# Selective-scan layer of a four-layer image network: softplus operations of POOL moved behind the products of their unit, three buffers for h and two for its product with C

## The chip, the cores and the metric

The kernel runs on one core of a Trainium2 chip, in one launch. The metric is the device time of that launch in microseconds, as the median of several runs. The engines are called as the profile calls them: PE (TensorE), DVE (VectorE), ACT (ScalarE), POOL (GpSimd) and SP (SyncE, which here only issues DMAs).

## What is computed

The network has four layers, each of the form `x = x + layer(group_norm(x))`, on `x` of shape 2 x 192 x 96 x 96 in float32: a deformable convolution, a Laplacian with a 1x1 convolution, a bidirectional RWKV recurrence, and a selective scan. Only the last one is touched. Cut to what matters, it is this, with L = 9216 places in a row per image, 384 inner channels and 16 states per channel:

```python
xz = x_flat @ W_in.T                       # 192 -> 768
x_in, z_gate = split(xz, 2)
x_conv = silu(causal_conv4(x_in) + conv_b) # 4 taps per channel
dt, B_ssm, C_ssm = split(W_x @ x_conv, [12, 28])
delta = softplus(W_dt @ dt + 2 * b_dt)
A = -exp(A_log)
# for every place t, channel d, state n:
h = exp(delta * A) * h + (delta * x_conv) * B_ssm
y = sum_n(h * C_ssm) + D * x_conv
out = W_out @ (y * silu(z_gate))
```

## The kernel before

The place axis is cut into 38 steps (19 per image: 17 of 511 places and two of 264 or 265). The work of a step on the recurrence is cut into 12 **units**, numbered q = 0 to 11: three blocks of 128 channels (index i), each in four parts (index v). A unit holds 32 channels x 16 states, as 128 partitions (16 states by 8 channels) with 4 rows in the free dimension (index r). So a loop over k = 0 to 455 runs over all units, with step s = k // 12 and q = k % 12.

Work on a unit, with the lines of the kernel:

- `load` (L2336, SP): a 1022 KB DMA brings `delta * x_conv` from the DRAM tensor `ud`, repeated over the states, into `bu` (pool `sc`, four buffers). ACT copies the state that the step before left into its first column (L2340).
- `times_b` (L2346, POOL): `bu` times the row of B, in place.
- `steps_of` (L2356, PE): four small matmuls spread delta over the states into PSUM banks `da`. There are five such banks for four rows, so those of unit q+1 need banks that the scan of unit q frees.
- `decay` (L2370, ACT): `da = exp(A * delta)`, in place in PSUM, four operations.
- `scan` (L2379, DVE): four `tensor_tensor_scan` operations write `h` (pool `sb`, two buffers) from `da` in PSUM and `bu`.
- `times_c` (L2403, DVE): rows 0 to 2 of `h` times the row of C in PSUM, into `hc` (pool `s3`, three buffers).
- `times_c_aside` (L2414, POOL): row 3 of `h` times the same row in SBUF, into `hp` (pool `s3`).
- `sum_of` (L2427, PE): sums `hc` and `hp` over the states into the PSUM bank `acc`; at v = 0 it begins with the term of D (L2421).
- `gate` (L2440, DVE), after each fourth unit: `acc` times the gate.
- `keep` (L2386, ACT): the last column of `h` becomes the state.

Beside the units, three generators make the rest, one piece at each call of `go`. `early(s + 2)` makes normalization, input projections (L2242), convolution (L2262) and SiLU for two steps ahead. `late(s + 1)` makes the small projections, softplus and `ud` for the next step. `output(s - 1)` makes the output projection (L2452) and adds the residual (`xr`, L2460). Their matmuls share one PSUM bank, `pe`, so that each waits for the copy of the one before.

The softplus part of `late` is `relu(a) + log(1 + exp(-|a|))` with a correction for rounding. After ACT's Exp (L2310) and the addition of one (L2311), the pieces are: one of DVE (L2313) with ACT's Ln behind it (L2314), and then three of POOL, each on 128 x 1533 elements:

```python
nc.vector.scalar_tensor_tensor(du, ln, -1.0, du, ALU.add, ALU.subtract)   # L2313
nc.scalar.activation(ln, ln, AF.Ln)                                       # L2314
yield
nc.gpsimd.tensor_tensor(ln, ln, du, ALU.subtract)                         # L2316
yield
nc.gpsimd.tensor_tensor(dl, dl, ln, ALU.add)                              # L2318
yield
nc.gpsimd.tensor_tensor(du, dl, us, ALU.mult)                             # L2320
```

L2320 is followed by four DMAs from SP that write `ud` (L2322), which the loads of the next step read.

The order on PE, ACT, DVE and POOL is the order in which the program is written (`manual_schedule`); SP's order is the framework's. In iteration k the loop writes: `sum_of(k - 2)`, `scan(k)`, `steps_of(k + 1)`, `decay(k + 1)`, `times_c(k)`, `gate` if due, at q = 4 to 7 a piece of `late`, then `times_c_aside(k - 1)`, `times_b(k + 2)`, `load(k + 3)` and `keep(k)`, with pieces of the generators between by tables (`AHEAD`, `BEHIND`). Counting the calls, the piece with L2313 and Ln falls on q = 4, and those with L2316, L2318 and L2320 on q = 5, 6 and 7. On POOL the order of units 5 to 7 is therefore: the softplus operation, `hp` of unit q - 1, `times_b` of unit q + 2.

Of the kernel before, what the change touches and what calls it, by code (L numbers as in the profile page):

```python
# [6 lines left out]
F32 = mybir.dt.float32  # L7
# [11 lines left out]
P = 128  # L19
# [44 lines left out]
class Net:  # L64
# [2021 lines left out]
    def layer3(self, x, out, stats):  # L2086
# [4 lines left out]
        TM = 511  # L2091
# [8 lines left out]
        with ExitStack() as ctx:  # L2100
            wp = ctx.enter_context(tc.tile_pool(name="w3", bufs=1))
            s1 = ctx.enter_context(tc.tile_pool(name="l3s", bufs=1))
            sb = ctx.enter_context(tc.tile_pool(name="l3", bufs=2))
            s3 = ctx.enter_context(tc.tile_pool(name="l3h", bufs=3))
# [102 lines left out]
            steps = []  # L2207
# [120 lines left out]
            def where(k):  # L2328
                return k // NQ, k % NQ, k % NQ // NV, k % NV
# [13 lines left out]
            def times_b(k):  # L2343
                s, q, _, _ = where(k)
                bu = got[s]["bu", q][:, :, 1:]
                nc.gpsimd.tensor_tensor(  # L2346
                    bu, bu, got[s]["bs"].unsqueeze(1).to_broadcast([P, 4, steps[s][2]]), ALU.mult
                )

            def steps_of(k):  # L2350
                s, q, i, v = where(k)
                T = steps[s][2]
                das = [decays[(4 * k + r) % 5][:, : T + 1] for r in range(4)]
                for r in range(4):
                    at = slice(32 * r, 32 * r + 32)
                    nc.tensor.matmul(  # L2356
                        das[r][:, 1:],
                        spread[at, v].rearrange("p n e -> p (n e)"),
                        got[s]["dl"][at, i],
                        start=True,  # L2360
                        stop=True,
                        tile_position=(32 * r, 0),
                    )
                got[s]["da", q] = das

            def decay(k):
                s, q, _, _ = where(k)
                for r in range(4):
                    da = got[s]["da", q][r][:, 1:]
                    nc.scalar.activation(  # L2370
                        da, da, AF.Exp, scale=nA[:, 4 * q + r : 4 * q + r + 1]
                    )

            def scan(k):
                s, q, _, _ = where(k)
                h = sb.tile([P, 4, TM + 1], F32, name="h")[:, :, : steps[s][2] + 1]
                bu = got[s]["bu", q]
                for r in range(4):
                    nc.vector.tensor_tensor_scan(  # L2379
                        h[:, r], got[s]["da", q][r], bu[:, r], 0.0, ALU.mult, ALU.add  # L2380
                    )
                got[s]["h", q] = h

            def keep(k):
                s, q, _, _ = where(k)
                nc.scalar.copy(state[:, q], got[s]["h", q][:, :, steps[s][2]])  # L2386

            def rows_c(s):
                cc = ps.tile([P, TM], F32, name="cc")[:, : steps[s][2]]
                nc.tensor.matmul(  # L2390
                    cc,
                    pick.rearrange("p n e -> p (n e)"),
                    got[s]["xd"][:NST],
                    start=True,
                    stop=True,
                )
                got[s]["cc"] = cc

            def times_c(k):
                s, q, _, _ = where(k)  # L2400
                T = steps[s][2]
                hc = s3.tile([P, 3, TM], F32, name="hc")[:, :, :T]
                nc.vector.tensor_tensor(  # L2403
                    hc,
                    got[s]["h", q][:, :3, 1:],
                    got[s]["cc"].unsqueeze(1).to_broadcast([P, 3, T]),
                    ALU.mult,
                )
                got[s]["hc", q] = hc

            def times_c_aside(k):
                s, q, _, _ = where(k)
                hp = s3.tile([P, TM], F32, name="hp")[:, : steps[s][2]]
                nc.gpsimd.tensor_tensor(hp, got[s]["h", q][:, 3, 1:], got[s]["cs"], ALU.mult)  # L2414
                got[s]["hp", q] = hp

            def sum_of(k):
                s, q, i, v = where(k)
                if v == 0:
                    acc = ps.tile([P, TM], F32, name="acc")[:, : steps[s][2]]  # L2420
                    nc.tensor.matmul(  # L2421
                        acc, skip[:, i], got[s]["us"][:, i], start=True, stop=False
                    )
                    got[s]["acc"] = acc
                acc = got[s]["acc"]
                for r in range(4):
                    nc.tensor.matmul(  # L2427
                        acc[32 * r : 32 * r + 32],
                        gather[:, v],
                        got[s]["hc", q][:, r] if r < 3 else got[s]["hp", q],  # L2430
                        start=False,
                        stop=v == NV - 1,
                        tile_position=(0, 32 * r),
                    )

            def gate(k):
                s, q, i, v = where(k)
                if i == 0:
                    got[s]["y"] = s1.tile([P, ND, TM], F32, name="y")[:, :, : steps[s][2]]
                nc.vector.tensor_tensor(  # L2440
                    got[s]["y"][:, i], got[s]["acc"], got[s]["zs"][:, i], ALU.mult
                )

            def output(s):
                b, t0, T = steps[s]
                y = got[s]["y"]
                xr = s1.tile([CH, 2, TM], F32, name="xr")[:, :, :T]
                nc.sync.dma_start(out=xr, in_=halves(x[b])[:, :, t0 : t0 + T])
                for m in range(2):
                    pe = bank(T)  # L2450
                    for d in range(ND):
                        nc.tensor.matmul(  # L2452
                            pe[:CH],
                            w_out[:, d, m * CH : (m + 1) * CH],
                            y[:, d],
                            start=d == 0,
                            stop=d == ND - 1,
                        )
                    yield
                    nc.vector.tensor_tensor(xr[:, m], pe[:CH], xr[:, m], ALU.add)  # L2460
                    if m == 1:
                        nc.sync.dma_start(out=halves(out[b])[:, :, t0 : t0 + T], in_=xr)
                    yield
# [29 lines left out]
            def go(name):  # L2493
                next(running[name], None)

            for k in range(nk):
                s, q, _, _ = where(k)
                if q == 0 and s + 1 < ns:
                    running["late"] = late(s + 1)
                if q == 2 and s:  # L2500
                    running["out"] = output(s - 1)
                if q == 3 and s + 2 < ns:
                    running["early"] = early(s + 2)
                if q in AHEAD:
                    go(AHEAD[q])
                    go(AHEAD[q])
                if k >= 2:
                    sum_of(k - 2)
                if q == 0 and s:
                    rows_c(s)  # L2510
                scan(k)
                if q in (4, 5):
                    go("out")
                if k + 1 < nk:
                    steps_of(k + 1)
                if q in BEHIND:
                    go(BEHIND[q])
                if k + 1 < nk:
                    decay(k + 1)
                if q in BEHIND and BEHIND[q] != "out":  # L2520
                    go(BEHIND[q])
                if q == 3:
                    go("late")
                    go("early")
                times_c(k)
                if k >= 2 and (k - 2) % NV == NV - 1:
                    gate(k - 2)
                if q in (4, 5, 6, 7):
                    go("late")
                if q == 11:  # L2530
                    go("early")
                if k:
                    times_c_aside(k - 1)
                if k + 2 < nk:
                    times_b(k + 2)
                if k + 3 < nk:
                    load(k + 3)
                keep(k)
# [99 lines left out]
```

## Time and profile before

| | |
|---|---|
| median of 3 runs | 10368.99 us (10358.51 to 10370.72) |
| the profiled execution, its own time | 10352.81 us |
| span of its instructions | 10351.0 us, mean granted clock 0.915 |
| busy share PE, DVE, ACT, POOL | 88%, 79%, 59%, 67% |
| first and last scan (L2379) start | 7137.2 and 10341.5 us |
| in the stretch 7137 to 10343: PE, DVE, POOL, ACT busy | 3013, 2848, 2835, 1993 of 3206 us |
| in the same stretch: granted clock, DMA share | 0.89, 0.77 |

All times of rows are microseconds from the start of the span, unless marked ns. A row of the page's list of groups gives line, engine, operation, `out<-in`, shapes and count; then the busy time and the mean in ns of one; then the idle time of the engine just before these instructions and what ended most of it. A row of a timeline gives start, duration, engine, line, operation, names, shapes and count of neighbours merged; in brackets stand the engine's idle time before it and what ended that. A row of windows gives the stretch, its length, busy time and count of PE, its weight loads, DVE, ACT and POOL, and then the granted TensorE clock, the DMA share and GB/s.

### The profile page before, as it was taken

What the parts mean: (1) busy time and instruction counts of PE and PEld (TensorE: products, weight loads), DVE (VectorE), ACT (ScalarE), POOL (GpSimd) and SP (SyncE); (2) the same over time, 40 slices, a digit from 0 to 9 for tenths busy, and PEclk for the clock granted to TensorE, in tenths of its full rate; (3) what the DMA queues carried; (4) which work ended last, traced back from release to release, by engine and by line L of the source; (5) the groups of instructions that cost most, each with busy time, mean ns of one, the idle gap of its engine ahead of it and who ended that gap; (6) DMA issues with size and microseconds to landing.
All of it is one profiled execution on the core that took longest, in us unless ns stands there. A gap on an engine that the chain in (4) does not pass through costs nothing. (4 is left out here: it accounts for less than half of the span.)

```text
span 10351.0 us, 222379 instructions
## 1 busy us (share of the span) xinstructions
PE 9158.5 (88%) x87686; PEld 5342.5 (52%) x87686; DVE 8210.6 (79%) x8842; ACT 6081.6 (59%) x11850; POOL 6980.6 (67%) x5645
## 2 busy tenths in 40 slices
PE   4799999999979999999866777887999999999998
PEld 3587788787768888888722222223222222222223
DVE  5688878788677777777655789984889888888888
ACT  0366666666667677777500168664666666666665
POOL 1466666766666666666511268773888889988898
PEclk8899999999989999999978788887999999988898
DMA  8455555555434555555444344433787777878776
GB/s 148 91 139 135 136 136 139 137 136 134 119 90 128 136 136 138 139 137 138 109 131 129 117 149 159 130 118 83 172 176 172 172 174 173 173 173 172 174 170 149
DMA packets 877164, 1465.17 MB, mean 142 GB/s; under 512 B 251616, under 2 KB 682276, under 8 KB 875012
## 3 DMA queue, kind: packets, MB, share of 16 engines
q1 hardware_dynamic: 663276, 1264.09, 48.9%
q0 software_dynamic: 104000, 133.19, 5.8%
q10 hardware_dynamic: 108840, 53.57, 2.1%
q8 instruction: 701, 11.49, 0.5%
q14 instruction: 347, 2.84, 0.1%
HBM read 871.06 MB, written 381.46 MB: 121 GB/s over the span
## 5 line engine op out<-in xcount | busy, mean ns | idle before, releaser
L2379 DVE TENSOR_TENSOR_SCAN h<-da,bu 128x512 f32<-128x512 f32 (+2 forms) x1824 | 1981.6, 1148 | 374.0 <-POOL hp L2414 200.1
L581 DVE TENSOR_TENSOR sp<-h 128x2304 f32<-128x2304 f32 x790 | 2165.0, 2773 | 41.6 <-ACT h L560 41.6
L2346 POOL TENSOR_TENSOR bu<-bu,bs 128x2044 f32<-128x2044 f32 (+2 forms) x456 | 1958.3, 4295 | 66.0 <-DMA bu<-ud 53.0
L605 ACT COPY st<-pt 128x512 f32<-128x512 f32 (+1 forms) x2370 | 1213.6, 515 | 1100.8 <-PE pt L597 1029.4
L597 PE MATMUL pt<-ident,sp 128*128 128x128 f32 x14220 | 1674.8, 276 | 87.4 <-DVE sp L581 41.0
L603 DVE COPY st<-pt 128x512 f32<-128x512 f32 x1580 | 1063.7, 687 | 829.9 <-PE pt L597 810.7
L597 PEld LDWEIGHTS pt<-ident,sp 128*128 128x128 f32 x14220 | 1565.3, 142 | 169.9 <-issue 97.2
L551 POOL TENSOR_TENSOR h<-u,step 128x1152 f32<-128x1152 f32 (+1 forms) x474 | 1096.0, 2330 | 679.8 <-DVE u L524 480.8
L569 POOL DMA_DIRECT2D xw<-xp_d x2500 | 1389.9, 619 | 194.7 <-PE pt L648 82.5
L2370 ACT ACTIVATE da<-da,nA 128x511 f32<-128x511 f32 (+2 forms) x1824 | 1063.4, 638 | 595.0 <-PE da L2356 586.9
L648 PE MATMUL pt<-st,xw 64*32 64x288 f32 (+1 forms) x30000 | 1098.0, 371 | 141.8 <-DVE st L603 62.7
L674 ACT COPY val<-pt 128x288 f32<-128x288 f32 (+1 forms) x3000 | 958.0, 404 | 285.2 <-PE pt L648 259.9
L776 PE MATMUL pf<-main,wd 126*64 126x128 f32 (+1 forms) x17064 | 986.2, 274 | 9.7 <-DMA far_m<-val 9.4
L776 PEld LDWEIGHTS pf<-main,wd 126*64 126x64 f32 x17064 | 913.7, 140 | 155.9 <-issue 146.9
L2356 PE MATMUL da<-dl,spread 32*128 32x511 f32 (+2 forms) x3648 | 984.0, 643 | 6.7 <-DVE h L2379 6.7
L648 PEld LDWEIGHTS pt<-st,xw 64*32 64x32 f32 x30000 | 548.0, 107 | 556.6 <-ACT val L674 171.7
L2403 DVE TENSOR_TENSOR hc<-h,cc 128x1533 f32<-128x1533 f32 (+2 forms) x456 | 751.2, 1647 | 0.0
L797 PE MATMUL pf<-more,wl 118*64 118x144 f32 (+5 forms) x11592 | 737.9, 278 | 3.0 <-DMA more<-far_l 2.2
L797 PEld LDWEIGHTS pf<-more,wl 118*64 118x64 f32 (+1 forms) x11592 | 670.2, 137 | 71.1 <-issue 63.4
L2356 PEld LDWEIGHTS da<-dl,spread 32*128 32x128 f32 x3648 | 311.6, 192 | 674.7 <-DVE h L2379 396.1
L2414 POOL TENSOR_TENSOR hp<-h,cs 128x511 f32<-128x511 f32 (+2 forms) x456 | 553.4, 1214 | 99.6 <-DVE h L2379 48.1
L2242 PE MATMUL pe<-xn,sb_w_in 96*128 96x511 f32 (+2 forms) x912 | 527.1, 709 | 94.6 <-ACT xi L2250 37.1
(344 smaller groups left out, 13016.1 us busy)
## 6 DMA issues: line engine op xcount, KB each, us to landing
bu<-ud SPq DMA_DIRECT2D x408, 1022.0 KB
main<-val SPq DMA_DIRECT2D x2016, 91.1 KB
far_l<-val SPq DMA_DIRECT2D x288, 324.0 KB
xw<-xp_d POOLq DMA_DIRECT2D x2500, 26.0 KB
far_m<-val SPq DMA_DIRECT2D x288, 162.0 KB
half_d<-hv SPq DMA_DIRECT2D x54, 768.0 KB
hv<-half_d SPq DMA_DIRECT2D x54, 768.0 KB
more<-far_l SPq DMA_DIRECT2D x576, 60.8 KB
```

What stands on the lines that cost most here:

```text
L551: nc.gpsimd.tensor_tensor(hs, u[:, :, 8 * KK * l : 8 * KK * l + n].unsqueeze(3).to_broadcast([P, 2, n, WS]), con["step"].unsqueeze(1).unsq ...
L569: nc.gpsimd.dma_start(out=xw[e * WN : (e + 1) * WN, i], in_=xp_d[y : y + WS, x : x + WS, e * CM // 2 : e * CM // 2 + XW],)
L581: nc.vector.tensor_tensor(sp.rearrange("p s (y x) -> p s y x", x=WS), hy.unsqueeze(3).to_broadcast([P, n, WS, WS]), hx.unsqueeze(2).to_bro ...
L597: nc.tensor.transpose(pt[:, q], sp[:, 2 * (q0 + q) : 2 * (q0 + q) + 2].rearrange("p e w -> p (e w)"), self.ident,)
L603: nc.vector.tensor_copy(st[:, q0 : q0 + m], pt[:, :m])
L605: nc.scalar.copy(st[:, q0 : q0 + m], pt[:, :m])
L648: nc.tensor.matmul(to, xw[e * WN : (e + 1) * WN, win, g * CG : g * CG + 32], sts[pair][e * WN : (e + 1) * WN].rearrange("p s (r c) -> p s ...
L776: nc.tensor.matmul(place(cv, m, 2 - t // 3, 2 - t % 3, None, 0), con["wd"][:, cv, t, m * CO : (m + 1) * CO], blocks(took, 1, rows), start= ...
L797: nc.tensor.matmul(place(cv, m, 2 * cv if alone else 1 - cv, 2 - t, h, 1 - alone,), con["wl"][lanes, slot, t, m * CO : (m + 1) * CO], bloc ...
L2346: nc.gpsimd.tensor_tensor(bu, bu, got[s]["bs"].unsqueeze(1).to_broadcast([P, 4, steps[s][2]]), ALU.mult)
L2356: nc.tensor.matmul(das[r][:, 1:], spread[at, v].rearrange("p n e -> p (n e)"), got[s]["dl"][at, i], start=True, stop=True, tile_position=( ...
L2379: nc.vector.tensor_tensor_scan(h[:, r], got[s]["da", q][r], bu[:, r], 0.0, ALU.mult, ALU.add)
```

## The change

The tile `h` comes from the pool with three buffers and `hc` from the one with two. At q = 4 nothing moves; at q = 5, 6 and 7 the piece of `late` is written behind `times_c_aside(k - 1)` and `times_b(k + 2)` and ahead of `load(k + 3)`. No instruction is added or removed.

```diff
             def scan(k):
                 s, q, _, _ = where(k)
-                h = sb.tile([P, 4, TM + 1], F32, name="h")[:, :, : steps[s][2] + 1]
+                h = s3.tile([P, 4, TM + 1], F32, name="h")[:, :, : steps[s][2] + 1]
...
             def times_c(k):
                 s, q, _, _ = where(k)
                 T = steps[s][2]
-                hc = s3.tile([P, 3, TM], F32, name="hc")[:, :, :T]
+                hc = sb.tile([P, 3, TM], F32, name="hc")[:, :, :T]
...
                 times_c(k)
                 if k >= 2 and (k - 2) % NV == NV - 1:
                     gate(k - 2)
-                if q in (4, 5, 6, 7):
+                if q == 4:
                     go("late")
                 if q == 11:
                     go("early")
                 if k:
                     times_c_aside(k - 1)
                 if k + 2 < nk:
                     times_b(k + 2)
+                if q in (5, 6, 7):
+                    go("late")
                 if k + 3 < nk:
                     load(k + 3)
                 keep(k)
```

## The prediction

> **What bounds the kernel now.** I read the page first, then the timelines of single engines through one step of the last layer, then two stretches with the granted clock. The page:
>
> ```profile
> span 10351.0 us, 222379 instructions
> ...
> DVE  5688878788677777777655789984889888888888
> ...
> L2379 DVE TENSOR_TENSOR_SCAN h<-da,bu 128x512 f32<-128x512 f32 (+2 forms) x1824 | 1981.6, 1148 | 374.0 <-POOL hp L2414 200.1
> ```
>
> The last layer is the last 12 slices, and DVE is the busiest there beside PE. Its scan idled 374.0 us, 200.1 of them because POOL had not finished hp of two units earlier: with two buffers, scan of unit q may not overwrite h before hp of unit q-2 has read it. I write S5 for the scan of unit 5 of a step, and likewise hp4, times_b7, hc4. Now DVE in one step of twelve units (S0 at 8322.94, next S0 at 8412.59), and POOL beside it:
>
> ```profile
> 8350.57 4.56 DVE L2379 TENSOR_TENSOR_SCAN h<-da,bu 128x512 f32<-128x512 f32 x4
> 8355.17 0.69 DVE L2460 TENSOR_TENSOR xr<-pe,xr 96x511 f32<-96x511 f32 x1
> 8355.78 1.74 DVE L2403 TENSOR_TENSOR hc<-h,cc 128x1533 f32<-128x1533 f32 x1
> 8357.44 1.75 DVE L2313 SCALAR_TENSOR_TENSOR du<-ln,du 128x1533 f32<-128x1533 f32 x1
> 8359.10 4.56 DVE L2379 TENSOR_TENSOR_SCAN h<-da,bu 128x512 f32<-128x512 f32 x4
> 8363.58 0.66 DVE L2460 TENSOR_TENSOR xr<-pe,xr 96x511 f32<-96x511 f32 x1
> ...
> 8376.23 4.57 DVE L2379 TENSOR_TENSOR_SCAN h<-da,bu 128x512 f32<-128x512 f32 x4 [2.87 <-POOL hp L2414]
> ...
> 8385.30 4.57 DVE L2379 TENSOR_TENSOR_SCAN h<-da,bu 128x512 f32<-128x512 f32 x4 [2.86 <-POOL hp L2414]
> ```
> ```profile
> 8350.89 4.52 POOL L2346 TENSOR_TENSOR bu<-bu,bs 128x2044 f32<-128x2044 f32 x1 [0.47 <-DMA bu<-ud]
> 8362.48 3.43 POOL L2316 TENSOR_TENSOR ln<-ln,du 128x1533 f32<-128x1533 f32 x1 [7.07 <-ACT bu L2340]
> 8365.87 1.25 POOL L2414 TENSOR_TENSOR hp<-h,cs 128x511 f32<-128x511 f32 x1
> 8367.09 4.50 POOL L2346 TENSOR_TENSOR bu<-bu,bs 128x2044 f32<-128x2044 f32 x1
> ```
>
> S4, S5, S7 and S8 are shown. In unit 5 POOL stands 7.07 us: the softplus subtraction L2316 is ahead of hp4 and times_b7 and needs ACT's Ln (8360.92 to 8362.40), which needs DVE's L2313. Then each of units 5 to 7 has a 3.4 us softplus operation ahead of its hp, and S6, S7, S8 wait 0.66, 2.87 and 2.86. In 34 steps that is 200 us.
>
> What ends last after xr of unit 5 (done at 8364.24) is another thing: a PE and ACT sequence through one PSUM bank, project, copy, project, copy, taps, with the decays between, up to S1 of the next step (8420.21). PE waits for DVE only where it needs a bank of da that a scan frees:
>
> ```profile
> 8364.29 3.11 PE L2242 MATMUL pe<-xn,sb_w_in 96*128 96x511 f32 x4 [0.58 <-DVE xr L2460]
> ...
> 8377.28 3.58 PE L2356 MATMUL da<-dl,spread 32*128 32x511 f32 x8
> ...
> 8384.01 3.77 PE L2242 MATMUL pe<-xn,sb_w_in 96*128 96x511 f32 x4 [0.67 <-ACT zs L2257]
> ```
>
> So a step is two pieces in series: DVE without a gap from S2 to xr of unit 5, then PE and ACT from xr to the next S1. Steps come in three kinds in turn, 86.3, 86.9 and 89.7 us (mean 87.6), with tails from xr of 53.7, 53.4 and 56.0 us.
>
> **Part 1: h with three buffers, hp ahead of softplus.** S7 then waits for hp4, done at about 8356.7. All 200 us of waits for hp go, but in the tail only what PE waits for counts. In the step from 8236.63 this is one place, L2356 for unit 9 at 8297.73: 3.41 us where a free one takes 1.14. That is 2.27, of which 0.44 is lost again because the next copy then waits for ACT's decays: 1.83. In the step from 8149.78 the same place took 2.80: 1.66 less 0.49, 1.17. In the step shown it is the 3.58 above: 2.44. There the granted clock was half from 8382.1 to 8388.9, after that wait, and cost more: the L2242 before and at 8384.01 took 2.54 and 3.77 against 1.98, the eight L2427 1.56 against 0.99. If that half clock goes with the wait, it is 2.9 more less 0.3 of waits for copies, 5.1 in all. Mean of the three kinds: 1.8 if the half clock stays, 2.7 if it goes. I take 2.4, nearer the upper end, because the wait ahead of that half clock is what is removed.
>
> **Part 2: hc with two buffers.** hc of unit q now waits for sum_of of unit q-2 (PE L2427). Set against the timeline, sum_of ends 0.6 to 1.4 us after hc1 now starts, and in unit 9 later by 1.3 to 2.2. In unit 9 DVE's gate has to wait for the same matmuls anyway, and PE is the bound. In unit 1 DVE has a gap of 0.1 (with 0.6) or 0.9 (with 1.3 to 1.4) ahead of S2 that takes some of it: 0.46 are left, and DVE has no gap from there to xr, so they count. Behind hc in the queue are gate and the next scan. +0.46.
>
> **Part 3: what fills POOL's 7 us.** In the new order hp4 and times_b7 lie in the stretch where POOL stood. POOL is free at 8355.41, hp4 takes 1.25, the load of unit 7's bu landed at 8355.79 (chain in order of time), so times_b7 runs from 8356.65 to 8361.15. DVE's L2313 would start at 8357.44, inside it. L2313 reads two tensors in SBUF, as no other DVE operation of this loop does (scan, hc, gate and xr have one input in PSUM). Now it always falls where POOL waits for it, at 1.75 us each time. What happens otherwise is seen in layer 1, with the same kind of operation:
>
> ```profile
> 5809.49 4.58 DVE L1579 SCALAR_TENSOR_TENSOR t<-pad,pair 96x1536 f32<-96x1536 f32 x1 [3.07 <-POOL pair L1576]
> ...
> 5816.25 1.74 DVE L1579 SCALAR_TENSOR_TENSOR t<-pad,pair 96x1536 f32<-96x1536 f32 x1
> ```
> ```profile
> 5806.43 6.03 POOL L1576 TENSOR_TENSOR pair<-pad 96x1649 f32<-96x1649 f32 x2 [18.95 <-DVE y L1603]
> ```
>
> Beside POOL's second L1576 (to 5812.46) L1579 took 4.58 instead of 1.74: it ended as if begun 0.13 us before POOL's end. The one L2313 of the loop that met a times_b, near the end (10198.52, half length), took 2.41 against 0.98, again ending as if begun 0.13 before POOL's end (10200.08). So L2313 starts effectively at 8361.02: +3.58 here, +3.46 in the step from 8149.78, +4.2 in that from 8236.63, where POOL comes to hp4 later. Bounds: 0 if L2313 gets in first (then POOL waits 1.75 and has room), 4.4 if both start together. I take 3.5. It lies on the gapless piece: L2313 is followed by S5, xr and the tail; ACT's Ln and L2316 shift too, but decays of unit 6 come at 8367 and S6 could not start before 8370.
>
> [...]
>
> **Part 4: the rest, at nothing.** POOL has the same 5,645 instructions. L2320 and its four ud DMAs on SP come some 2 us later after S4 than now; the load of unit 11 behind them (8387.00) would land about 8396, its times_b end at 8400, S11 needs it at 8406. The cover is 5 us or more; if gone, each us late is 34 us in all. Other loads move with the scans that free bu.
>
> **Sum.** Per step 3.5 + 0.46 - 2.4 = +1.56, times 34 = +53. The profiled execution took 10352.8 (span 10351.0 and 1.8 around it), 16 under the median of the three runs, 10369.0. 10352.8 + 53 = 10406, and with the 16: 10422, rounded to 10420.
>
> [...]
>
> ```profile
> 8190.90:8197.80 6.90, 6.90 (x14) 2.03 (x14) 6.90 (x7) 1.05 (x4) 6.90 (x3) 0.51 0.80 185
> ...
> 8365.00:8368.40 3.40, 3.40 (x5) 0.98 (x4) 2.74 (x4) 2.06 (x6) 3.40 (x3) 0.50 0.62 160
> ```
>
> At the start of the tail the clock (last figure but two) was half for 6.9 us in one step and 3.4 in another, each with PE (second figure) fully busy. [...]
>
> **Rivals.** (a) *L2313 gets in first*, and the change does what its words suggest: -2.4 + 0.46 = -1.9 per step, -66, 10303; with the tail's gain at 2.7 or 1.8, 10293 to 10323. For it: times_b7 would lead by only 0.1 to 0.9 us. It decides if POOL reaches times_b7 more than 2.2 us after S4's end. Against: hp4 can start at S4's end and the load was there 0.2 to 0.8 after it in nearly every step. 0.15. (b) *It meets in part*: one kind of step in three, that of 8236.63 with its lead near 0.1, escapes; +2.3 + 0.46 - 2.4, 12 us, 10381. 0.19. (c) *It meets and the clock loses too*: PE idles 3.5 us longer ahead of xr, the gain is 1.2 or less; +2.8 per step, 10463. Within the forecast's sign. Forecast with (c): 0.66.
>
> **The numbers.** What a measurement can tell from no change is about 0.2%, 21 us. Faster 0.15, within 0.19, slower 0.66. The range leaves out most of (a) and little above (c): 10330 to 10470. The forecast's own range, from 3.4 and 2.7 to 4.2 and 1.8 for the two terms, is 10408 to 10466.
>
> **What would show it.** Right: scan's idle <-POOL hp near zero; L2313 a mean near 5.2 us with times_b beside it; POOL's wait before L2316 shorter than 7 us; S7 and S8 idle behind ACT da instead; hc waiting for PE in unit 1. Wrong: L2313 still at 1.75 us, or L2356 for units 8 and 9 above 1.2 us.

## The result and the profile after

The changed kernel took 10386.87 us (median of 20 runs, 10366.80 to 10400.13) against 10359.33 us (20 runs of the kernel before, 10343.03 to 10376.12). The ratio is 1.0028, with a 95% interval of 1.0021 to 1.0035. So it is slower, as forecast, and inside the range, but the loss is 27.5 us where 51 had been forecast against the three runs shown. The profiled execution is the fastest of the 20 (10366.80): it lies 14.0 us above the one of before.

First the page after: its span, DVE's slices, and the groups of scan and of `hc`.

```profile
span 10365.0 us, 222647 instructions
...
DVE  5788888788677777777655789884999999999999
...
L2379 DVE TENSOR_TENSOR_SCAN h<-da,bu 128x512 f32<-128x512 f32 (+2 forms) x1824 | 1979.8, 1146 | 102.6 <-ACT da L2370 86.3
...
L2403 DVE TENSOR_TENSOR hc<-h,cc 128x1533 f32<-128x1533 f32 (+2 forms) x456 | 755.1, 1656 | 171.3 <-PE acc L2427 169.3
```

Scan no longer idles for `hp`: 374.0 us of idle time became 102.6, and the releaser is ACT. A new wait has come, 171.3 us of `hc` for `sum_of`. And DVE's slices of the last layer have gone from 8 up to 9: it is busier in about the same span, with no work added. The timelines of DVE and POOL through S4 to S8 of one step show where (S0 at 9292.6, next at 9381.4):

```profile
9320.10 4.55 DVE L2379 TENSOR_TENSOR_SCAN h<-da,bu 128x512 f32<-128x512 f32 x4
9324.58 0.66 DVE L2460 TENSOR_TENSOR xr<-pe,xr 96x511 f32<-96x511 f32 x1
9325.16 1.74 DVE L2403 TENSOR_TENSOR hc<-h,cc 128x1533 f32<-128x1533 f32 x1
9326.82 5.48 DVE L2313 SCALAR_TENSOR_TENSOR du<-ln,du 128x1533 f32<-128x1533 f32 x1
9332.23 4.55 DVE L2379 TENSOR_TENSOR_SCAN h<-da,bu 128x512 f32<-128x512 f32 x4
...
9345.96 4.57 DVE L2379 TENSOR_TENSOR_SCAN h<-da,bu 128x512 f32<-128x512 f32 x4
...
9352.98 4.57 DVE L2379 TENSOR_TENSOR_SCAN h<-da,bu 128x512 f32<-128x512 f32 x4
```
```profile
9324.80 1.27 POOL L2414 TENSOR_TENSOR hp<-h,cs 128x511 f32<-128x511 f32 x1 [0.36 <-DVE h L2379]
9326.18 4.51 POOL L2346 TENSOR_TENSOR bu<-bu,bs 128x2044 f32<-128x2044 f32 x1
9333.90 3.41 POOL L2316 TENSOR_TENSOR ln<-ln,du 128x1533 f32<-128x1533 f32 x1 [3.21 <-ACT bu L2340]
```

`times_b7` starts at 9326.18, L2313 at 9326.82, and L2313 takes 5.48 us in place of 1.75: it ends 1.61 after POOL's end at 9330.69, which is 1.74 less 0.13. S7 and S8 start without a wait of their own. POOL's wait ahead of L2316 fell from 7.07 to 3.21. All L2313 of the layer (minimum, median, maximum in ns; before, the median was 1746):

```profile
L2313 DVE SCALAR_TENSOR_TENSOR du<-ln,du x38: 985/5344/9252, 7101.7 to 10282.2; 128x1533 f32<-128x1533 f32 x34, 128x795 f32<-128x795 f32 x2, 128x792 f32<-128x792 f32 x2
```

The mean time from each scan to the next over steps 2 to 34 (33 full steps), worked out from the start times in the traces, is the comparison by place. E1 is the first experiment below.

| from scan to next | S0 | S1 | S2 | S3 | S4 | S5 | S6 | S7 | S8 | S9 | S10 | S11 | step |
|---|---|---|---|---|---|---|---|---|---|---|---|---|---|
| before | 7.61 | 7.46 | 6.15 | 6.12 | 8.42 | 7.57 | 8.54 | 9.08 | 6.13 | 7.87 | 6.58 | 6.13 | 87.66 |
| after | 7.54 | 7.40 | 6.12 | 6.12 | 12.13 | 7.31 | 6.39 | 6.97 | 7.01 | 9.15 | 6.33 | 6.12 | 88.57 |
| E1 | 7.58 | 7.71 | 6.12 | 6.12 | 8.49 | 7.31 | 6.48 | 7.02 | 8.37 | 7.83 | 6.18 | 6.12 | 85.32 |

After the change, S6 and S7 go on 2.15 and 2.11 us sooner, S8 and S9 give back 0.88 and 1.28, because PE is the bound there (hc8 and hc9 wait 0.64 and 2.31 us a step for PE's `sum_of`), and S4 to S5 pays 3.71 for L2313. In the two pieces of the prediction: DVE from S1 to xr of unit 5 went from 33.27 to 36.89, the tail from 54.34 to 51.63.

### The profile page after: what moved, and what is told of

Read it like the earlier page. It is cut to its first block, busy times and chain, and to the rows that moved or that the text cites. A ratio compares the mean times of both kernels' runs of the same rounds, so it can differ in the third digit from the quotient of the medians.

```text
span 10365.0 us, 222647 instructions
## 1 busy us (share of the span) xinstructions
PE 9044.9 (87%) x87686; PEld 5317.9 (51%) x87686; DVE 8345.7 (81%) x8842; ACT 6080.6 (59%) x11850; POOL 6997.7 (68%) x5645
## 5 line engine op out<-in xcount | busy, mean ns | idle before, releaser
L2379 DVE TENSOR_TENSOR_SCAN h<-da,bu 128x512 f32<-128x512 f32 (+2 forms) x1824 | 1979.8, 1146 | 102.6 <-ACT da L2370 86.3
L2356 PE MATMUL da<-dl,spread 32*128 32x511 f32 (+2 forms) x3648 | 927.3, 659 | 117.7 <-DVE h L2379 117.6
L2403 DVE TENSOR_TENSOR hc<-h,cc 128x1533 f32<-128x1533 f32 (+2 forms) x456 | 755.1, 1656 | 171.3 <-PE acc L2427 169.3
L2356 PEld LDWEIGHTS da<-dl,spread 32*128 32x128 f32 x3648 | 297.9, 195 | 708.3 <-DVE h L2379 491.0
```

The lines of the kernel that those rows point to most:

```text
L2356: nc.tensor.matmul(das[r][:, 1:], spread[at, v].rearrange("p n e -> p (n e)"), got[s]["dl"][at, i], start=True, stop=True, tile_position=( ...
L2379: nc.vector.tensor_tensor_scan(h[:, r], got[s]["da", q][r], bu[:, r], 0.0, ALU.mult, ALU.add)
```

## The experiments

Each was timed in five rounds beside the kernel before on the same chip. The experiments came in batches on different chips, and the medians of before differ a little (10345 to 10359), so ratios are compared; they have 95% intervals. The diffs of E1 to E4 and E7 are against the changed kernel, those of E8 and E12 against the kernel before, and those of E5, E6 and E9 to E11 against E1.

**E1, the buffers without the move.** The piece of `late` goes back ahead of `hp` and `times_b`.

```diff
-                if q == 4:
+                if q in (4, 5, 6, 7):
                     go("late")
...
-                if q in (5, 6, 7):
-                    go("late")
```

> The buffers of the change (h three, hc two), POOL's order as before. Theory 1 (the loss is L2313, held while POOL's hp4 and times_b7 run beside it, +3.6 us on DVE's piece of a step; the gain is the tail from xr to the next S1, 54.3 to 51.6 us, and comes from h's third buffer alone): L2313 stays at 1.75 us, POOL still stands 5 to 7 us ahead of L2316, scan's wait for hp is near zero, a step is about 85.3 us, ratio to before about 0.992. Theory 2 (the loss is hc's two buffers, whose 171 us of waits for PE's sums are new): ratio like the whole change, 1.003.

Measured: 10269.95 us (10256.94 to 10283.02), ratio 0.9923 [0.9910, 0.9937]. Scan's row on its page, and L2313:

```profile
L2379 DVE TENSOR_TENSOR_SCAN h<-da,bu 128x512 f32<-128x512 f32 (+2 forms) x1824 | 1980.7, 1147 | 153.8 <-ACT da L2370 100.1
```
```profile
L2313 DVE SCALAR_TENSOR_TENSOR du<-ln,du x38: 972/1743/3686, 7104.9 to 10197.5; 128x1533 f32<-128x1533 f32 x34, 128x795 f32<-128x795 f32 x2, 128x792 f32<-128x792 f32 x2
```

The waits for `hp` are gone without the move, since a third buffer of `h` frees S7 from hp5 whatever stands ahead of it on POOL. POOL stands idle at L2313 again and L2313 is back at 1.74 (in three of the 33 full steps a late times_b6 held it, 1.96 to 3.69). So the gain comes from the buffers and the loss from the move. This version beats both kernels.

**E2, the move with L2313's second input in PSUM.** Everything of the change stays; L2313 reads `cc` (PSUM, same shape) instead of `du`, times zero, wherever both have the same length (33 of the 38 steps). This leaves out the rounding correction of softplus.

```diff
-                nc.vector.scalar_tensor_tensor(du, ln, -1.0, du, ALU.add, ALU.subtract)
+                other = got[s - 1].get("cc") if s else None
+                if other is not None and steps[s - 1][2] == T:
+                    nc.vector.scalar_tensor_tensor(
+                        du, ln, 0.0, other.unsqueeze(1).to_broadcast([P, ND, T]), ALU.mult, ALU.mult
+                    )
+                else:
+                    nc.vector.scalar_tensor_tensor(du, ln, -1.0, du, ALU.add, ALU.subtract)
```

> The whole change, but L2313 reads its second input from PSUM (the row of C) instead of SBUF, with a product by zero; the rounding correction of softplus is so left out, nothing else. Theory 1: L2313 is 1.75 us beside times_b7, which stays at 4.5 us, the piece from S1 to xr falls from 36.9 to 33.3 us, a step is about 85.3 us, ratio about 0.992. Theory 2: L2313 is of no account, ratio 1.003.

Measured: 10268.61 us, 0.9927 [0.9913, 0.9940]. The row of the operation, which has times_b7 beside it as after the change:

```profile
L2315 DVE SCALAR_TENSOR_TENSOR du<-ln,cc x33: 1736/1741/1746, 7298.8 to 10023.2; 128x1533 f32<-128x1533 f32 x33
```

The longest of 33 is 1746 ns. With the order as changed, moving one operand out of SBUF takes the whole loss away (step 85.13). So L2313 was held where both its inputs lay in SBUF while POOL's times_b7 ran: 5344 ns in the median after the change, 1741 here. I call this the lock. The expectations below speak of a port that the two engines share; no run shows more of a port than such times.

**E3, the move alone** (`h` two buffers, `hc` three, the pieces behind).

```diff
-                h = s3.tile([P, 4, TM + 1], F32, name="h")[:, :, : steps[s][2] + 1]
+                h = sb.tile([P, 4, TM + 1], F32, name="h")[:, :, : steps[s][2] + 1]
...
-                hc = sb.tile([P, 3, TM], F32, name="hc")[:, :, :T]
+                hc = s3.tile([P, 3, TM], F32, name="hc")[:, :, :T]
```

> POOL's new order alone, h with two buffers and hc with three as before. Theory 1: L2313 held as in the whole change (5.3 us), and since S6 comes 3.6 us later, hp is early enough for two buffers: scan's waits for hp under 40 us in all, hc waits for nothing, ratio 1.000 to 1.003. Theory 2: without hc's waits the whole gain of the order shows, ratio 0.992.

Measured: 10357.90 us, 1.0015 [1.0006, 1.0024]. Its scan row:

```profile
L2379 DVE TENSOR_TENSOR_SCAN h<-da,bu 128x512 f32<-128x512 f32 (+2 forms) x1824 | 1981.5, 1148 | 251.7 <-ACT da L2370 229.6
```

The move by itself also ends the waits for `hp` (the releaser is ACT) and gets the tail to 51.89, against 51.72 in E1 and 51.63 after. So move and buffers are two ways to the same gain. Only the move pays 5.21 us for L2313.

**E4, the change with `hc` at three buffers** (room for it from `xt`, which gets one buffer).

```diff
-                xt = sb.tile([CH, 2, TM], F32, name="xt")[:, :, :T]
+                xt = s1.tile([CH, 2, TM], F32, name="xt")[:, :, :T]
...
-                hc = sb.tile([P, 3, TM], F32, name="hc")[:, :, :T]
+                hc = s3.tile([P, 3, TM], F32, name="hc")[:, :, :T]
```

> The whole change with three buffers for hc as well (room for them comes from xt, which gets one buffer instead of two). Theory 1: hc's waits go, but they lie where PE is the bound or L2313 hides them: 0 to 15 us less than the whole change, ratio 1.001 to 1.003. Theory 2: ratio 0.992 or less.

Measured: 10370.89 us, 1.0024 [1.0013, 1.0035], against 1.0028 for the change. The wait of `hc` went (171.3 to 0.3 us), and the ACT wait of scan took its place (86.3 to 242.8):

```profile
L2379 DVE TENSOR_TENSOR_SCAN h<-da,bu 128x512 f32<-128x512 f32 (+2 forms) x1824 | 1981.5, 1148 | 253.4 <-ACT da L2370 242.8
```

A step took 88.65 against 88.57: the third buffer of `hc` is worth nothing here. What the single buffer of `xt` costs was not run by itself.

**E5, E11, E6: one, two and three products more on DVE, in E1.** To see what a microsecond in the DVE piece costs, operations of 128x511 with one input in PSUM, like the L2313 that POOL did not hold in E2 (1746 ns at most), were put behind hc4. They take 0.69 us each, and each puts L2313 off by 0.72.

```diff
                 times_c(k)
+                for _ in range(1 if q == 4 else 0):     # 2 in E11, 3 in E6
+                    nc.vector.tensor_tensor(
+                        got[s]["hc", q][:, 0], got[s]["h", q][:, 0, 1:], got[s]["cc"], ALU.mult)
```

> e1 (buffers of the change, POOL's old order) with one product of 128x511 done again on DVE in unit 4 of each step (0.6 us, one input in PSUM, between S4 and L2313). Theory W (a step fits itself to a whole number of TensorE clock windows of 3.41 us, as the 85.33 = 25 and 88.75 = 26 windows of the runs so far suggest: xr later in its window means less of the tail at half clock): the step stays at 85.33 us, the piece S1 to xr grows by 0.6 and the tail shrinks by as much; same time as e1, ratio 0.992. Theory A (additive): step 85.95, 20 us more than e1, ratio 0.994.

> e1 with two products of 128x511 done again on DVE in unit 4 (1.2 us). One such left a step at 85.33 us, three made a mean of 87.6 in a pattern of three steps to 77 windows. Theory W (steps in few windows to few steps): 25.5 windows, 87.04 us, or still 85.33; ratio 0.992 or 0.998 to 0.999. Theory A (additive above 0.6): 85.9 to 86.6, ratio 0.994 to 0.996.

> The same with three such products in unit 4 (1.9 us). Theory W: the tail can't give back that much, and the step goes to 88.75 us (26 windows) or a mixture of 85.33 and 88.75; ratio 1.000 to 1.003, which is as much as L2313 held for 3.6 us costs. Theory A: step 87.2, 63 us more than e1, ratio 0.998.

Measured: 0.9923 [0.9910, 0.9937], 0.9959 [0.9947, 0.9972] and 0.9992 [0.9983, 1.0001], against 0.9923 of E1. The mean steps are 85.39, 86.49 and 87.61, against 85.32. So the first 0.72 us cost 0.07, and then each 0.72 costs about 1.1. Work put on the DVE piece does lengthen the step, as the prediction has it for the lock, but not by its own length. Of the two theories in the expectations, W was met by E5, and E11 came out in the range of A; E6 lies between the two. In E5 23 of the 33 full steps lie within 0.02 us of 85.33; in E1 13 do, and 22 within 0.1. S4 of three steps in a row, in E1:

```profile
9183.94 4.56 DVE L2379 TENSOR_TENSOR_SCAN h<-da,bu 128x512 f32<-128x512 f32 x4
...
9269.28 4.56 DVE L2379 TENSOR_TENSOR_SCAN h<-da,bu 128x512 f32<-128x512 f32 x4
...
9354.61 4.56 DVE L2379 TENSOR_TENSOR_SCAN h<-da,bu 128x512 f32<-128x512 f32 x4
```

They are 85.34 and 85.33 apart. In the traces of before and after, all 828 stretches of whole and of half granted clock but the last of each trace last whole multiples of 3.413 us, to 1 ns. I call this a window; 85.33 is 25 of them. In E6 the pattern is 88.36, 87.34, 87.12, together 77 windows for three steps, and before it was 86.3, 86.85, 89.65, also 77 for three. In E11 it is 85.88, 86.87, 86.66, 76 for three. After the change the typical step is 88.7, near 26 windows, and in E4 21 of 33 lie within 0.1 of 88.75, which is 26. This is an observation of lengths; no run set the windows apart from the kernel. The three pieces of 0.72 us cost 0.07, 1.10 and 1.12 us, next to nothing or about a third of a window (1.14).

**E7, the first of the three ahead.** L2316 ahead of hp4 and times_b7, so that POOL waits as before, and the other two pieces behind.

```diff
-                if q == 4:
+                if q in (4, 5):
                     go("late")
...
-                if q in (5, 6, 7):
+                if q in (6, 7):
                     go("late")
```

> The whole change, but L2316 stays ahead of hp in unit 5, so that POOL stands until Ln is there and L2313 has the port to itself; L2318 and L2320 go behind as in the change. Theory 1: L2313 1.75 us, step 85.3 us, ratio 0.992 or, with some of the 11 us that the change gains in the short second step, 0.991.

Measured: 10354.34 us, 1.0004 [0.9995, 1.0013]. The expected 1.75 us of L2313 and 85.3 of the step both failed: the step took 87.66. The group of L2313 in this run, and two of its waits between 7300 and 10300 (total, times, longest):

```profile
L2313 DVE SCALAR_TENSOR_TENSOR du<-ln,du x38: 975/3068/3598, 7102.6 to 10265.5; 128x1533 f32<-128x1533 f32 x34, 128x795 f32<-128x795 f32 x2, 128x792 f32<-128x792 f32 x2
```
```profile
POOL bu L2346 <- DMA bu<-ud: 143.3, 27, 8.8
...
DVE h L2379 <- POOL bu L2346: 92.0, 35, 8.0
```

Counted from L2316, L2320 and the four DMAs that write `ud` come 5.7 us later than in E1 (23.85 against 18.16), and SP issues the load of unit 11 behind them, 2.3 us after L2320 ends. times_b11 then waits for that load, S11 for times_b11, and POOL is late into the next step, where L2313 meets times_b6 (median 3.07). That is the cover of 5 us that Part 4 named, used up. So the queue of SP behind `ud` is a second price of moving these pieces. After the change itself, POOL's wait for loads is also 163.7 us (39.3 before), but scan's wait for `bu` is only 9.4, so there the cover held, with L2320 3.4 us later after S4 than before (the prediction had some 2).

**E8, `hc` with two buffers and nothing else.**

```diff
-                hc = s3.tile([P, 3, TM], F32, name="hc")[:, :, :T]
+                hc = sb.tile([P, 3, TM], F32, name="hc")[:, :, :T]
```

> The kernel before with two buffers for hc, nothing else. The prediction put +0.46 us a step on it, 15 us, ratio 1.0015. If the clock windows or DVE's gaps take it, 1.000.

Measured: 10341.70 us, 0.9989 [0.9980, 0.9998], a trace faster, and neither expectation. `hc` does wait for `sum_of` (117.4 us), S1 to S2 grew from 7.46 to 7.71 as Part 2 has it, but the tail shrank from 54.34 to 53.50 and the step from 87.66 to 87.01, which is 51 clock windows for two steps.

**E9 and E10, POOL's idle time of E1 filled with other work** at q = 5: ten short products (0.7 us), or ten memsets (0.52 us) of a spare tile.

```diff
+            aside = wp.tile([P, TM], F32, name="aside")
+            nc.gpsimd.memset(aside, 0.0)
...
+                for _ in range(5 if q == 5 else 0):        # E9
+                    nc.gpsimd.tensor_tensor(aside[:, :264], got[s]["cs"][:, :264], got[s]["bs"][:, :264], ALU.mult)
+                    nc.gpsimd.tensor_tensor(aside[:, 264:508], got[s]["cs"][:, :244], got[s]["bs"][:, :244], ALU.mult)
...
+                for _ in range(10 if q == 5 else 0):       # E10
+                    nc.gpsimd.memset(aside, 0.0)
```

> e1 (buffers of the change, POOL's old order) with ten short products of two SBUF tiles on POOL into a tile nobody reads, about 6.5 us, put where POOL stands idle ahead of L2316 in unit 5. Nothing waits for them and nothing is moved. Theory 1 (the port that L2313 and POOL share): L2313 is held until they end, 5 to 6 us instead of 1.75, a step 88.75 us (26 windows) and ratio 1.000 to 1.003, like the whole change. Theory 2 (order or buffers): POOL's idle time hides them, 85.33 us and 0.992.

> The same place with ten memsets of 128x511 on POOL, about 4.7 us, which read nothing. Theory 1: L2313 stays at 1.75 us beside them, step 85.33 us, ratio 0.992. If any busy POOL holds DVE: as with the products, 1.000 to 1.003.

E10 measured 0.9942 [0.9930, 0.9955], with L2313 at 1.75 beside the memsets in 30 of the 33 full steps (in the other three times_b6 ran late and held it):

```profile
L2531 POOL MEMSET aside<- x380: 513/523/548, 7160.9 to 10250.8; 128x511 f32 x190
```
```profile
L2315 DVE SCALAR_TENSOR_TENSOR du<-ln,du x38: 972/1746/4326, 7106.2 to 10195.3; 128x1533 f32<-128x1533 f32 x34, 128x795 f32<-128x795 f32 x2, 128x792 f32<-128x792 f32 x2
```

The ratio was expected at 0.992, and the step of 85.59 is 0.26 above E1's; why was not looked into. It is far from the 88.57 of the change. So a busy POOL is not by itself the cause: the memsets, which read nothing, took 548 ns at most beside an L2313 of 1.75 us. Of POOL's operations that read SBUF, times_b7 held L2313 (5344 ns in the median after the change), and the products of E9 were held beside it (up to 2871 ns, below).

E9 measured 1.0048 [1.0036, 1.0060], slower than expected, but for another reason than the one tested:

```profile
L2315 DVE SCALAR_TENSOR_TENSOR du<-ln,du x38: 972/1747/11194, 7095.4 to 10292.4; 128x1533 f32<-128x1533 f32 x34, 128x795 f32<-128x795 f32 x2, 128x792 f32<-128x792 f32 x2
```
```profile
DVE h L2381 <- POOL bu L2348: 147.5, 77, 2.9
```

Between short products L2313 mostly got in (median 1747) and POOL's product was held (2.2 to 2.9 us for 0.70). POOL reached times_b7 13.1 us after S4's end in place of 10.3, and scan waited 147.5 us for `bu`. So this run doesn't tell the lock's price.

**E12, `h` at three buffers and nothing else of the change** (`xt` at one, to fit).

```diff
-                h = sb.tile([P, 4, TM + 1], F32, name="h")[:, :, : steps[s][2] + 1]
+                h = s3.tile([P, 4, TM + 1], F32, name="h")[:, :, : steps[s][2] + 1]
...
-                xt = sb.tile([CH, 2, TM], F32, name="xt")[:, :, :T]
+                xt = s1.tile([CH, 2, TM], F32, name="xt")[:, :, :T]
```

> POOL's old order, three buffers for h and for hc (xt has one instead of two). No wait of hc for PE. Theory W: the step stays at 85.33 us, ratio 0.992, though 4 us of hc's waits per step go. Theory A: 0.3 to 0.5 us a step less than e1, ratio 0.990 to 0.991.

Measured: 10280.76 us, 0.9930 [0.9917, 0.9943], step 85.31 against E1's 85.32. From S1 to S2 it has 7.38 where E1 has 7.71, so the 0.33 of `hc`'s wait are there, and the step doesn't show them, as theory W had it. The gain is the third buffer of `h` alone.

## Why the prediction was right in its sign and too high

*The lock (Part 3), forecast +3.5, measured +3.73* (L2313 from 1.75 to 5.48 in the mean of the full steps). The cause (E2: 1741 ns with one input in PSUM), its place and its size were right. Rival (a), that L2313 gets in first, came true in five of the 33 full steps, and these are 84.6 to 85.8 long, like E1's. Rival (b), that one kind of step in three escapes, did not. But the condition given for (a) was wrong. It said that L2313 is free if POOL reaches times_b7 more than 2.2 us after S4's end. In the 12 steps where it did (2.35 to 5.31), hp4 or a late times_b6 went first, times_b7 close behind still went ahead of L2313, and L2313 took 6.3 to 9.3 us. In the five that escaped POOL reached times_b7 1.6 to 1.8 us after S4. The long ones offset the ones that escaped.

*The tail (Part 1), forecast -2.4, measured -2.71.* The working had 2.7 for the case that the half clock goes with the wait, and the forecast took less. That the half clock made the difference isn't shown: by the clock records of the full steps, the tail spent 10.7 us at half clock before, 8.7 after the change, but 10.2 in E1, whose tail is as short. The working also counted too few waits. It took one L2356 in each step, 2.12 us in the mean above the free 1.14. But the 3.58 of the step shown there belongs to unit 8, not to unit 9 as in the other two, and unit 7 took 2.03 beside it. In the mean of the full steps L2356 for units 7, 8 and 9 fell from 1.46, 2.06 and 2.56 to 1.14 each, 2.66 in all. For unit 9 of the step shown under the result it took 1.14, whole clock:

```profile
9358.08 1.14 PE L2356 MATMUL da<-dl,spread 32*128 32x511 f32 x8
```

Windows of the tail, from xr of unit 5 to the next S1, first the kernel before (of the step shown in the prediction), then after (the step above); the columns are the stretch, its length, busy time of PE, its loads, DVE, ACT, POOL, the granted clock, DMA share and GB/s:

```profile
8364.24:8420.21 55.97, 53.14 (x169) 16.39 (x170) 46.24 (x39) 29.72 (x58) 55.46 (x21) 0.87 0.73 166
```
```profile
9337.28:9388.97 51.69, 48.12 (x170) 15.44 (x170) 46.47 (x39) 28.06 (x56) 46.98 (x18) 0.90 0.78 180
```

Rival (c), that the clock loses while PE waits for the held L2313, did not come. The clock does go to half in that wait, for 10.24 us from 9332.67, three windows where E1 has two. But half of it lies ahead of the end of xr (9337.36): 5.6 us are in the tail, and E1 has 6.1 there. So the tail is 51.6 and 51.7.

*`hc` (Part 2), forecast +0.46, measured nothing in the step. This is the step of the prediction that failed.* `hc` waits for `sum_of` in unit 1 and beyond, as said (0.58 us a step in unit 1). In pairs that differ in `hc` (E8 and before; E1 and E12, and after and E4, where `xt` differs too) the DVE piece without L2313 is 0.18, 0.33 and 0.17 longer with two buffers. The step changes by -0.65, +0.02 and -0.08. So the premise failed that such a wait counts in full because DVE has no gap from there to xr. E5 shows the same: 0.72 us of work in that piece cost 0.07. After the change not even the piece shows the wait: the move starts unit 2 sooner (S1 to S2 is 7.19 in E3, 7.46 before), with both it is 7.40, and the whole rest of the DVE piece came out at -0.11. Why the step swallows so little as 0.3 us but not the 3.7 of L2313 is open; the windows above are an explanation that no run isolated.

*The sum.* Forecast +1.56 per step. Measured: +3.73, -0.11 and -2.71, which is +0.91, or 30 us in 33 steps in place of 51. The `hc` term is too high by 0.57, which is 19 us, and the tail's gain too small by 0.31, which is 10; the lock was taken 0.23 too low, which gives back 8.

*What the sum left out.* It took all steps as the full ones. Step 1 has units of 264 or 265 places with a full softplus beside them. It fell from 76.3 to 64.9 us in the profiled pair, at a granted clock of 0.78 and 0.89. With -4.6 from the rest (the start of the layer -2.5, step 0 -1.8, the last two steps and what follows -0.3), that is 30 less 16, the 14 of the pair. In the profiled runs of the four kernels with POOL's old order and nothing added (before, E1, E8, E12) step 1 took 76 to 80, in the ten others 65 to 72. That is one execution of each, so whether the edits decide it is open. Without step 1 the pair would differ by 25, near the 27.5 of the medians; that this is why the medians differ by more is argued, not shown. The allowance of 16 us from the profiled run to the median was also too much: over 20 runs that median is 6.5 above it.

*Part 4* held: S11 waits for `bu` 0.20 us a step after the change. E7 shows how near it was.

*The signs.* Of the five signs of being right four came. S7 and S8 don't idle behind ACT; in their place hc7 and hc8 wait for `sum_of`, 0.61 and 0.64 us a step.

## What to carry to other kernels

Before idle time of an engine is filled, look at what ran without hindrance because that engine stood still. Here, with a third buffer of `h`, POOL's wait of 5.5 us cost a step 0.2 us at most (85.32 in E1, against 85.13 in E2, where POOL doesn't wait there), and it was in this wait that L2313, with two operands in SBUF, took 1.74 us in E1 (median), against 5.34 after the change. And if the same wait can be ended by a buffer and by a new order, try each alone: the buffer gave 0.9923, the order 1.0015, both together 1.0028.

## What the runs showed of the hardware that was not expected

Between times_b and L2313 a lead of about half a microsecond in the recorded starts decided in these traces which of the two went first, and POOL, once first, mostly stayed so over neighbouring operations. In one step of the changed kernel L2313 came 0.56 us after times_b7 began and still went first. It took 1.75, and times_b7 6.67 in place of 4.51:

```profile
7379.25 1.27 POOL L2414 TENSOR_TENSOR hp<-h,cs 128x511 f32<-128x511 f32 x1 [0.28 <-DVE h L2379]
7380.71 6.67 POOL L2346 TENSOR_TENSOR bu<-bu,bs 128x2044 f32<-128x2044 f32 x1 [0.18 <-issue]
```
```profile
7381.27 1.75 DVE L2313 SCALAR_TENSOR_TENSOR du<-ln,du 128x1533 f32<-128x1533 f32 x1
```

In the step shown under the result the lead was 0.64, and POOL went first. In the traces of the change, E3 and E4 together, 13 meetings of times_b and L2313 had a lead between 0.3 and 0.6: DVE went first in nine, POOL in four. With 0.63 and more POOL always did (24 meetings in the full steps of the changed kernel, counting those in which hp4 or times_b6 was first). Where hp4 was first, POOL stayed ahead at shorter leads too: 0.30 to 0.54 in six meetings of the three traces. So by the recorded starts, which need not be the times of issue, times_b went first in every meeting only from a lead of 0.63 us on. In all 28 held cases of a full step of the changed kernel L2313 ended as if begun 0.13 us before POOL's end. Where hp4 held L2313, times_b7 behind it held it on, and so did hp4 behind a late times_b6 in six of seven meetings of full steps in these three traces, while between the products of 0.7 us in E9 L2313 mostly got in (median 1.75 us). What lies behind the half microsecond was not tried.

The second is that the steps fall in with the windows of the granted clock: 25 of 3.413 us in most steps of E1, E5 and E12 and half of those of E10, 51 for two steps in E8, 76 for three in E11, 77 for three before and in E6. A PE that was busy stayed at half clock for longer than two of them (6.83 us): here are two stretches in a row of the step shown under the result, with PE (second figure) busy all through 8.0 us at half clock, by the profile's account of busy:

```profile
9333.50:9337.70 4.20, 4.20 (x6) 1.47 (x6) 4.20 (x5) 3.68 (x7) 3.80 (x2) 0.50 0.00 0
9337.70:9341.50 3.80, 3.80 (x6) 1.73 (x6) 3.80 (x4) 0.66 (x1) 3.80 (x2) 0.50 0.71 154
```
